# Contexts, Wk, Wv and turned rows read from DRAM by transfers over all 128 partitions

## The chip, the cores and the metric

The kernel runs on one core of a Trainium2 chip. The metric is device time in microseconds: the median of three executions, 770.59 us for the kernel before (770.08 to 770.86). A profile is of one execution more.

Names used below: TensorE (PE; its weight loads are PEld), VectorE (DVE), ScalarE (ACT), GpSimd (POOL), and SyncE (SP), which computes nothing and issues most of the DMA transfers. The transfers themselves are carried by the core's 16 DMA engines. SBUF is the on-chip memory of 128 partitions; PSUM takes TensorE's results.

## The reference

A layer of cross attention and then a feed-forward product, for 16 batches of 128 tokens with 1024 features, in float32:

```python
x = x + xattn(layernorm(x), ctx, ctx, Wq, bq, Wk, bk, Wv, bv, Wo, bo)   # 32 query heads, 8 key/value heads of 32
x = x + scale * (ei(layernorm(x)) @ kernel)    # kernel is 0/1; ei scales the last 20% of the features by -4
```

`xattn` is `Q = q Wq + bq`, `K = c Wk + bk`, `V = c Wv + bv`, per head `softmax(Q K^T / sqrt(32)) V`, and the result times `Wo` plus `bo`. Wq and Wo are 1024 x 1024, Wk and Wv 1024 x 256.

## The kernel before

**Work in groups of two batches.** There are eight groups. For each: K and V of the two contexts, Q of the two normalized x, attention in four parts (two batches, two halves of the heads), the output product with Wo and the residual, a second normalization, and the feed-forward product. From the second or third group on, the products Q, K with V, output and feed-forward are each made from seven products of half-size blocks (`seven`, L569) instead of eight, with sums and differences of the weights' blocks prepared once and kept in DRAM.

**Operands stand transposed.** The products need contexts and x with features on the partitions. VectorE's transpose instruction turns blocks of 32 x 32 (L445, L471, L983). So that a tile of tokens x features becomes features x tokens, the blocks must be placed beforehand: block (token block t, feature block k) has to lie in partitions 32k to 32k+31, at place t. A transfer from DRAM does that placing:

- `load_ctx` (L161) brings a context, 128 tokens x 1024 features, into a tile `[128 partitions, 4 token blocks, 8 chunks, 32]`.
- `through_dram` (L394) does the same for rows that the kernel has computed itself: it stores the normalized rows to DRAM (L409) and reads them back placed (L406). `rows_x` uses it for the queries of groups 2 to 7 (tiles `turn_x`), the output product's normalization for the feed-forward input of groups 0 to 6 (tiles `turn_f`). SyncE waits at L406 until the store has landed.
- `load_by_quadrants` (L169) loads Wv and Wk, whose rows are permuted in the same way.

Each of the three works by quadrant: one transfer per feature block k writes partitions 32k to 32k+31, over all four token blocks or several feature chunks at once. In all there are 16 contexts, 12 turned x and 14 turned f tiles of 512 KB in four transfers of 128 KB each, and Wv and Wk of 1 MB each. Every piece that is contiguous on both sides is 1 KB.

**The head.** Before anything can be computed, contexts 0 and 1, Wv and Wk are loaded by three queues in turn, SyncE, ScalarE and GpSimd (L201 to L205). Then SyncE loads x of batches 0 and 1 (L183), the bias bo, six pieces of Wq, contexts 2 and 3, and more. GpSimd makes the identity for TensorE's transposes and loads the small biases. TensorE's order is V of batch 0, V of batch 1, K of both, transposes of x, Q (L418, L434).

**The order of the rest** is written out by a small planner, class `Stream` (L24): generators yield pieces of TensorE's work with an estimated time, and other steps are filed for a later point of that clock (`later`). The resulting order on each engine is fixed at build time. SyncE's queue is served in order: a transfer that has to wait for a buffer or for a landing holds up all behind it. Weights of Wq, Wo and their sums come as pieces of 512 KB through a ring of 8 buffers (`fetch`, L238, issue at L243), each fetched when TensorE has used up an older one. The rows turned through DRAM share two buffers named `turn` with incoming x.

Of the kernel before, what the change touches and what calls it, by code (L numbers as in the profile page):

```python
# [95 lines left out]
def kernel(  # L96
# [16 lines left out]
    nc = tc.nc  # L113
# [7 lines left out]
    NC = D // P  # L121
# [21 lines left out]
    wk_sb = const.tile([P, NC, KV], FP, name="wk_sb")  # L143
    wv_sb = const.tile([P, NC, KV], FP, name="wv_sb")
# [13 lines left out]

    NB = P // 32

    def load_ctx(b, queues=(nc.sync,)):  # L161
        c_t = work.tile([P, NB, NC, 32], FP, tag="ctx", name=f"ctx{b}", bufs=2)
        src = key_value[b].rearrange("(t r) (k c f) -> k r t (c f)", r=32, k=NB, c=NC)
        for k in range(NB):
            dst = c_t[k * 32 : (k + 1) * 32].rearrange("r t c f -> r t (c f)")
            queues[k % len(queues)].dma_start(out=dst, in_=src[k])
        cs[b] = c_t

    def load_by_quadrants(dst, w, queues, *cuts):  # L169

        src = w.rearrange("(k c f) n -> k f c n", k=NB, f=32)
        n = 0
        for lo, hi in zip((0,) + cuts, cuts + (NC,)):
            for k in range(NB):
                queues[n % len(queues)].dma_start(
                    out=dst[k * 32 : (k + 1) * 32, lo:hi], in_=src[k][:, lo:hi]
                )
                n += 1

    def load_x(b, tag="row"):  # L180

        x_t = work.tile([P, D], FP, tag=tag, name=f"xn{b}", bufs=2)
        nc.sync.dma_start(out=x_t, in_=x[b])  # L183
        xns[b] = x_t
        if tag == "turn":
            turning.add(f"xn{b}")
# [11 lines left out]

    three = (nc.sync, nc.scalar, nc.gpsimd)  # L201
    load_ctx(0, three)
    load_by_quadrants(wv_sb, Wv, (nc.scalar, nc.gpsimd, nc.sync), 2, 4)
    load_ctx(1, three)
    load_by_quadrants(wk_sb, Wk, (nc.scalar, nc.gpsimd, nc.sync), 4)  # L205
    load_x(0)
    load_x(1)
    ident = const.tile([P, P], FP, name="ident")
# [185 lines left out]
    def through_dram(row, name, store, back, turn, then, tag="turn"):  # L394

        there = dram.tile([P, D], FP, name=f"dram_{name}")

        def load():
            bufs = 2 if tag == "turn" else TB
            c_t = work.tile([P, NB, NC, 32], FP, tag=tag, name=f"turn_{name}", bufs=bufs)  # L400
            if tag == "turn":
                turning.add(name)
            src = there.rearrange("(t r) (k n) -> k r t n", r=32, k=NB)
            for k in range(NB):
                dst = c_t[k * 32 : (k + 1) * 32].rearrange("r t c f -> r t (c f)")
                nc.sync.dma_start(out=dst, in_=src[k])  # L406
            stream.later(turn - back, lambda: then(c_t))

        stream.later(store, lambda: nc.sync.dma_start(out=there, in_=row) and None)  # L409
        stream.later(back, lambda: stream.when(lambda: tag != "turn" or len(turning) < 2, load))  # L410
# [718 lines left out]
    with tc.manual_schedule():  # L1129
# [17 lines left out]
        for j in range(GB):  # L1147
            load_ctx(GB + j)
# [83 lines left out]
        for grp in range(NGRP):  # L1232
# [39 lines left out]
            if not more:  # L1272
                for q in range(2 * NA):
                    b, a = grp * GB + q % GB, q // GB
# [6 lines left out]
            for q in range(2 * NA):  # L1281
                b, a = grp * GB + q % GB, q // GB
# [65 lines left out]
```

## Time and profile before

| | |
|---|---|
| Median of 3 executions | 770.59 us |
| Profiled execution | 765.46 us, of it 763.7 us from the first to the last instruction (the span) |
| TensorE busy | 746.6 us, 98% of the span |
| VectorE, ScalarE, GpSimd busy | 541.5, 380.2, 303.2 us |
| Moved by DMA | 203.36 MB, mean 266 GB/s over the span |
| SyncE's queue (q1) | 102480 packets, 200.31 MB, their time 81.8% of that of 16 engines |
| Granted TensorE clock | 1.00 throughout |

How to read the profile's views: a line of groups gives source line, engine, operation, tiles as out<-in, count, and busy time. A line of waits reads "who waited <- for what: us in total, times, longest us". The chain of waits is followed back from the last instruction, each line being start, duration and what it was. A row of DMA by stretch of time gives the packets in it, the bytes, and the mean rate. The DMA share is the time that packets took divided by that of 16 engines; it can exceed 1, because packets overlap on an engine.

### The profile page before, as it was taken

What the parts mean: (1) busy time and instruction counts of PE and PEld (TensorE: products, weight loads), DVE (VectorE), ACT (ScalarE), POOL (GpSimd) and SP (SyncE); (2) the same over time, 40 slices, a digit from 0 to 9 for tenths busy, and PEclk for the clock granted to TensorE, in tenths of its full rate; (3) what the DMA queues carried; (4) which work ended last, traced back from release to release, by engine and by line L of the source; (5) the groups of instructions that cost most, each with busy time, mean ns of one, the idle gap of its engine ahead of it and who ended that gap; (6) DMA issues with size and microseconds to landing.
All of it is one profiled execution on the core that took longest, in us unless ns stands there. A gap on an engine that the chain in (4) does not pass through costs nothing.

```text
span 763.7 us, 14898 instructions
## 1 busy us (share of the span) xinstructions
PE 746.6 (98%) x5232; PEld 563.4 (74%) x5232; DVE 541.5 (71%) x961; ACT 380.2 (50%) x1397; POOL 303.2 (40%) x356
## 2 busy tenths in 40 slices
PE   4999999999999999999999999999999999999997
PEld 3888884699747996489855998469984699546466
DVE  1456888977787667677676687865778766769586
ACT  0245764444735455344643447434464455568363
POOL 4069830342740146401652226322274113108582
PEclk9999999999999999999999999999999999999999
DMA  9989999989499895999779995899948988752912
GB/s 229 311 319 295 372 372 412 324 272 347 158 326 267 283 319 173 316 261 294 253 244 294 297 292 201 282 314 272 316 165 297 274 274 266 240 194 83 286 45 110
DMA packets 104314, 203.36 MB, mean 266 GB/s; under 512 B 8960, under 2 KB 58432, under 8 KB 104240
## 3 DMA queue, kind: packets, MB, share of 16 engines
q1 hardware_dynamic: 102480, 200.31, 81.8%
q10 hardware_dynamic: 1248, 1.11, 0.7%
q0 software_dynamic: 512, 0.99, 0.6%
q8 instruction: 41, 0.67, 0.4%
q14 instruction: 33, 0.27, 0.1%
HBM read 170.40 MB, written 31.98 MB: 265 GB/s over the span
## 4 chain that ended last, share of the span: by engine, by line
PE 90%; DVE 7%; DMA 2%; issue 1%; ACT 0%; SPq 0%; DVEq 0%
PE q_u L558 13%; PE o_u L862 12%; PE f_u L1017 7%; PE tpp L802 7%; PE q_v L558 7%; PE o_v L862 7%; PE k_u L558 5%; PE sc L769 4%; PE av L811 4%; PE q L418 4%; PE f_v L1017 3%; PE q_c L558 3%; PE k_v L558 3%; PE o_c L862 3%; PE f_c L1017 2%; PE k L418 2%
## 5 line engine op out<-in xcount | busy, mean ns | idle before, releaser
L785 ACT ACTIVATE p<-sc,negm 128x128 f32<-128x128 f32 x512 | 181.2, 370 | 147.3 <-DVE negm L781 73.1
L781 DVE TENSOR_REDUCE negm<-sc 128x4 f32<-128x512 f32 x128 | 86.9, 682 | 72.5 <-PE sc L769 72.5
L356 POOL CAST wide<-wf_sb 128x512 fp32r<-128x512 int8 x154 | 109.2, 749 | 64.0 <-PE f_u L1017 62.7
L804 ACT COPY pt<-tpp 128x512 f32<-128x512 f32 x128 | 75.1, 595 | 96.9 <-PE tpp L802 96.3
L797 DVE TENSOR_TENSOR p<-p,inv 128x512 f32<-128x512 f32 x128 | 103.4, 808 | 4.4
L785 ACT ACTIVATION_READ_ACCUMULATOR p<-sc,negm 128x1 f32 x512 | 106.3, 208 | 0.0
L196 POOL TENSOR_TENSOR x<-x,bo_b 128x256 f32<-128x256 f32 x64 | 50.3, 806 | 87.6 <-DMA x<-in_x_dram 74.9
L558 PE MATMUL q_u<-t,piece 128*128 128x128 f32 x672 | 81.3, 275 | 0.0
L558 PEld LDWEIGHTS q_u<-t,piece 128*128 128x128 f32 x672 | 78.1, 192 | 0.2 <-issue 0.2
L802 PE MATMUL tpp<-ident,p 128*128 128x128 f32 x512 | 75.9, 273 | 1.6 <-DVE p L797 1.6
L802 PEld LDWEIGHTS tpp<-ident,p 128*128 128x128 f32 x512 | 61.3, 141 | 20.1 <-issue 13.6
L862 PE MATMUL o_v<-piece,s 128*128 128x512 f32 x128 | 60.6, 601 | 0.2 <-DVE x L876 0.2
L862 PE MATMUL o_u<-piece,s 128*128 128x512 f32 x128 | 59.7, 597 | 0.5 <-DVE x L876 0.5
L862 PE MATMUL o_u<-piece,yT 128*128 128x512 f32 x128 | 58.6, 599 | 0.0
L819 ACT ACTIVATE yT<-av,bvT 128x512 f32<-128x512 f32 x32 | 22.0, 688 | 60.3 <-PE av L811 60.3
L769 PEld LDWEIGHTS sc<-kv,qT 32*128 32x128 f32 x1024 | 31.5, 186 | 25.7 <-issue 25.7
L374 POOL TENSOR_TENSOR rs_f<-ve_f,minus_half 128x1 f32<-128x1 f32 x16 | 9.5, 595 | 96.1 <-DVE ve_f L372 83.0
L961 POOL TENSOR_TENSOR s<-turn_f,turn_f 128x512 f32<-128x512 f32 x7 | 8.9, 1277 | 97.3 <-DVE turn_f L983 71.0
L354 ACT CAST wide<-wf_sb 128x512 fp32r<-128x512 int8 x70 | 43.2, 633 | 3.3 <-PE f_u L1017 3.0
L862 PEld LDWEIGHTS o_u<-piece,yT 128*128 128x128 f32 x128 | 23.5, 190 | 28.4 <-issue 26.7
L862 PEld LDWEIGHTS o_u<-piece,s 128*128 128x128 f32 x128 | 23.0, 190 | 27.6 <-issue 22.7
L862 PEld LDWEIGHTS o_v<-piece,s 128*128 128x128 f32 x128 | 22.4, 190 | 23.3 <-issue 18.9
(155 smaller groups left out, 1493.0 us busy)
## 6 DMA issues: line engine op xcount, KB each, us to landing
piece<-o SPq DMA_DIRECT2D x64, 512.0 KB, 4.8
piece<-q SPq DMA_DIRECT2D x56, 512.0 KB, 7.1
piece<-in_L_xattn_Wq_dram SPq DMA_DIRECT2D x50, 512.0 KB, 8.0
piece<-in_L_xattn_Wo_dram SPq DMA_DIRECT2D x48, 512.0 KB, 7.1
piece<-kv SPq DMA_DIRECT2D x18, 512.0 KB, 6.9
xn<-in_x_dram SPq DMA_DIRECT2D x16, 512.0 KB, 4.6
x<-in_x_dram SPq DMA_DIRECT2D x16, 512.0 KB, 5.1
ctx<-in_ctx_dram SPq DMA_DIRECT2D x60, 128.0 KB, 7.2
```

Of the source, the lines that this page charges most:

```text
L196: lambda cut=cut: nc.gpsimd.tensor_add(x_t[:, cut], x_t[:, cut], bo_b[:, cut]) and None,
L356: nc.gpsimd.tensor_copy(t, wf_sb[:, FFN[name], c])
L418: nc.tensor.matmul(mm, lhsT=lhsT, rhs=rhs, start=k == 0, stop=k == n - 1)
L558: nc.tensor.matmul(mm if part is None else mm[:, part], lhsT=lhsT, rhs=rhs, start=start and n == k == 0, stop=k == len(some) - 1, skip_gro ...
L769: nc.tensor.matmul(tiles[i][:, g], lhsT=qT[rows, g], rhs=kT[rows], start=True, stop=True,)
L781: nc.vector.tensor_reduce(negm, tile_, AX.X, ALU.max, negate=True)
L785: nc.scalar.activation(p[:, g], tile_[:, g], AF.Exp, bias=negm[:, g : g + 1], accum_out=total[:, g : g + 1],)
L797: nc.vector.tensor_mul(p, p, inv.unsqueeze(2).to_broadcast([P, NG, S]))
L802: nc.tensor.transpose(tp[:, g], p[:, g], ident)
L804: nc.scalar.copy(pt, tp)
L862: nc.tensor.matmul(mm, lhsT=lhsT[:, 2 * k + c], rhs=w[:, c], start=start and k == c == 0, stop=k == c == 1, skip_group_check=True,)
L1017: nc.tensor.matmul(mm, lhsT=part[:, c], rhs=w, start=start and c == n == 0, stop=c == HC - 1 and n == 1, skip_group_check=True,)
```

## The change

Contexts, turned rows, Wv and Wk are now read by transfers whose SBUF side is all 128 partitions. A context or a turned row has one transfer per token block t (four of 128 KB, as many as before), Wv and Wk one per feature chunk c (eight of 128 KB each; Wv had twelve, eight of 64 KB and four of 128 KB). The DRAM side of such a transfer is four blocks k of 32 rows of 1 KB. Which data ends up where in SBUF is the same, and the order of instructions on the compute engines is the same. The first loads are issued by SyncE and ScalarE in turn, GpSimd issues none of them any more.

```diff
+    def blocks_in(dst, src, queues=(nc.sync,)):
+        src = src.rearrange("(t r) (k n) -> t k r n", r=32, k=NB)
+        for t in range(NB):
+            queues[t % len(queues)].dma_start(
+                out=dst[:, t].rearrange("p c f -> p (c f)"), in_=src[t]
+            )
+
     def load_ctx(b, queues=(nc.sync,)):
         c_t = work.tile([P, NB, NC, 32], FP, tag="ctx", name=f"ctx{b}", bufs=2)
-        src = key_value[b].rearrange("(t r) (k c f) -> k r t (c f)", r=32, k=NB, c=NC)
-        for k in range(NB):
-            dst = c_t[k * 32 : (k + 1) * 32].rearrange("r t c f -> r t (c f)")
-            queues[k % len(queues)].dma_start(out=dst, in_=src[k])
+        blocks_in(c_t, key_value[b], queues)
         cs[b] = c_t
 
-    def load_by_quadrants(dst, w, queues, *cuts):
-
-        src = w.rearrange("(k c f) n -> k f c n", k=NB, f=32)
-        n = 0
-        for lo, hi in zip((0,) + cuts, cuts + (NC,)):
-            for k in range(NB):
-                queues[n % len(queues)].dma_start(
-                    out=dst[k * 32 : (k + 1) * 32, lo:hi], in_=src[k][:, lo:hi]
-                )
-                n += 1
+    def load_rows(dst, w, queues):
+
+        src = w.rearrange("(k c f) n -> c k f n", k=NB, f=32)
+        for c in range(NC):
+            queues[c % len(queues)].dma_start(
+                out=dst[:, c], in_=src[c]
+            )
...
-    three = (nc.sync, nc.scalar, nc.gpsimd)
-    load_ctx(0, three)
-    load_by_quadrants(wv_sb, Wv, (nc.scalar, nc.gpsimd, nc.sync), 2, 4)
-    load_ctx(1, three)
-    load_by_quadrants(wk_sb, Wk, (nc.scalar, nc.gpsimd, nc.sync), 4)
+    two = (nc.sync, nc.scalar)
+    load_ctx(0, two)
+    load_rows(wv_sb, Wv, two)
+    load_ctx(1, two)
+    load_rows(wk_sb, Wk, two)
...
-            src = there.rearrange("(t r) (k n) -> k r t n", r=32, k=NB)
-            for k in range(NB):
-                dst = c_t[k * 32 : (k + 1) * 32].rearrange("r t c f -> r t (c f)")
-                nc.sync.dma_start(out=dst, in_=src[k])
+            blocks_in(c_t, there)
             stream.later(turn - back, lambda: then(c_t))
```

## The prediction

> **What bounds the kernel now.** I read the page's busy times first, then the chain of waits, then the DMA rows by stretch of time.
>
> ```profile
> PE 746.6 (98%) x5232; PEld 563.4 (74%) x5232; DVE 541.5 (71%) x961; ACT 380.2 (50%) x1397; POOL 303.2 (40%) x356
> DMA  9989999989499895999779995899948988752912
> q1 hardware_dynamic: 102480, 200.31, 81.8%
> PE 90%; DVE 7%; DMA 2%; issue 1%; ACT 0%; SPq 0%; DVEq 0%
> ```
>
> TensorE is busy 746.6 of 763.7 us; only 17 us are left. But the DMA engines are nearly as full (the second line, tenths in 40 slices). So a faster transfer can gain little, while a slower one soon has TensorE waiting. The chain of waits says where those few DMA microseconds are:
>
> ```profile
> 2.12 5.02 DMA wv_sb<-in_L_xattn_Wv_dram
> 7.16 7.83 DMA ctx<-in_ctx_dram
> 15.88 3.72 PE v L418 x16
> 19.60 6.92 PE k L418 x32
> ```
>
> All in the head: the first product waits for Wv until 7.13, the second batch for its context until 15.06, then V, K, and Q from 28.6 us.
>
> Next the DMA rows: 20 to 29 us (Wq pieces: 1 KB runs into 128 partitions), 30 to 34 us (contexts: 1 KB runs into 32 partitions), 113 to 119 us (4 KB runs), and one round of the main loop, 300 to 387 us.
>
> ```profile
> DMA packets 3152, 3.15 MB, mean 350 GB/s; under 512 B 96, under 2 KB 3146, under 8 KB 3152
> ...
> DMA packets 932, 0.86 MB, mean 216 GB/s; under 512 B 105, under 2 KB 931, under 8 KB 931
> ...
> DMA packets 1109, 2.42 MB, mean 404 GB/s; under 512 B 105, under 2 KB 105, under 8 KB 1108
> ...
> DMA packets 12203, 23.92 MB, mean 275 GB/s; under 512 B 1008, under 2 KB 7152, under 8 KB 12194
> ```
>
> The size of a run is the same in the first two rows; the shape of the transfer alone makes 350 or 216 GB/s. At 350 GB/s each of 16 engines carries 21.9 GB/s.
>
> **The change, part by part.** It touches 46 tiles of 512 KB (524,288 bytes): 16 contexts, 12 x rows and 14 f rows back from DRAM, and Wv and Wk, two each. A context or turned row still takes four transfers of 128 KB, Wv now 8 instead of 12, Wk 8 as before. What changes is each transfer's shape. Before, both sides begin with 32 rows. After, the SBUF side begins with 128 partitions and the DRAM side with the 4 column blocks (`t k r n`, `c k f n`).
>
> *Price of one transfer.* No transfer of before begins with fewer than 32, so I bound it. Low end: 16 engines share it as they share a Wq piece, 131,072 / 350 GB/s = 0.37 us, a tile in 1.50 us; today it is 524,288 / 216 = 2.43 us, so a tile gains 0.93 us of DMA time. High end: four engines share it, a block each: 131,072 / (4 x 21.9) = 1.50 us, a tile in 6.0 us on engines that every other transfer also needs, 3.6 us more than now. I take the high end. A share that an engine can copy alone must be cut out of the outermost dimension of both sides. The two rows above show that this dimension decides the rate. 4 is all that the DRAM side offers, and the Wq pieces that give the low end begin with 128 on both.
>
> The Trainium skill, page "DMA: Bandwidth & Descriptors", section "Why a DMA increments its semaphore by 16 and not by 1", speaks against this change: the number of engines is the largest up to 16 that divides the slowest non-unit dimension of both patterns, which for 4 and 128 is 4. By that rule the sum is the 845 us below, by the Wq row it would be 765. No run here shows it yet.
>
> *Head.* 24 transfers (contexts 0 and 1, Wv, Wk) x 1.50 = 36 us from the first packets at 2.1 us: all of Wk at 38. x0 and x1 stand behind them on SyncE: at 404 GB/s 1.3 us each, so x0 lands at about 39.5. The two normalizations took from 20.05 to 26.43 on VectorE (6.4), transposes and copy to Q at 28.60 another 2.2: Q starts at 48.1, **+19.5 us**. K is no later: its last chunk lands at about 38 and the second half of K is 3.5 us. TensorE has nothing else to do, so all of it counts. GpSimd loses its nine transfers (about 5.1 us of issue) and builds the identity earlier; nothing waits for it before 26.13 us: 0. ScalarE issues 12 instead of 9 and SyncE 12 instead of 10 (the page of before has 0.3 to 0.45 us each, and they wait for earlier landings, as L175 and L166 do now). Behind ScalarE's stand its table load and the first K output, needed at 41 us in the new time: 0. Behind SyncE's stand x, bo and the Wq pieces, priced above.
>
> *28.6 to 150 us.* The table of stretches has a DMA share of 0.94, 1.00, 1.03 and 1.01 here: no idle engine time to spare. Four context tiles and the first turned rows, about 5.5 tiles x 3.6 = 20 us more on the four engines. Against it stand SyncE's waits for TensorE to free a piece buffer (6.6 us at 60 to 90, about 8 at 120 to 150) and the ring of 8 pieces. Ends 0 and 20; I take **+8**, nearer the row of waits.
>
> *Rounds of 87 us, five of them from 150 to 590 us.*
>
> ```profile
> 150.00:237.00 87.00, 86.52 (x631) 64.97 (x630) 65.27 (x118) 43.13 (x161) 38.13 (x46) 1.00 0.88 275
> 237.00:325.00 88.00, 88.00 (x664) 68.25 (x664) 63.09 (x115) 43.03 (x162) 33.52 (x41) 1.00 0.85 273
> 500.00:590.00 90.00, 89.54 (x670) 69.31 (x669) 64.67 (x119) 44.54 (x170) 33.46 (x41) 1.00 0.86 266
> 680.00:764.00 84.00, 78.22 (x341) 49.74 (x339) 62.67 (x100) 46.88 (x127) 46.31 (x59) 1.00 0.38 132
> ```
>
> (Columns: stretch, us, PE, PEld, DVE, ACT, POOL busy, clock, DMA share, GB/s.) A round moves 23.9 MB. Six tiles are 3.15; six Wq pieces, another 3.15, go at 350 GB/s, 9.0 us; 17.6 MB go at 404, 43.6 us. Those 52.6 us use all engines alike; on the four, six tiles add 36: **88.6 us in a round of 87**. TensorE can no longer hide them. And the four cannot be busy all the time: SyncE waits for each turned row's store before it loads it back and issues nothing meanwhile,
>
> ```profile
> SPq L406 <- DMA dram_f<-x2n: 9.3, 2, 7.1
> SPq L183 <- DVE x2l_s L933: 8.8, 1, 8.8
> SPq L406 <- DMA dram_x<-xq: 2.6, 1, 2.6
> ```
>
> (SyncE's waits, 300 to 387 us). Behind those L406 waits stand the next pieces of Wq, Wq's sums and Wo. I let a round have 7 us of such idle time: 95.6, about **+9 a round, +45 in all**. Ends: 0 (packets overlap as the 109.8% share at 20 to 29 us shows) and 6 x 3.6 = 21.
>
> *590 us to the end.* Four tiles in the first stretch: 21.5 MB / 404 = 53 us and 24 us, 77 of 90: +2. In the last, with a share of 0.38, two tiles: 0.
>
> Sum: 19.5 + 8 + 45 + 2 = 74.5. The profiled execution took 765.46 us, so 840; the median shown, 770.59, lies 5.1 us above it: **845 us**.
>
> **Rivals.**
> - *Faster: 16 engines share it after all.* For it: the Wq row. Against: the DRAM side's 4. The head's 24 transfers take 9 us: x1 by 14.7, norms 6.4, Q at about 23.5 instead of 28.6. Elsewhere TensorE is at 99 to 100% and 0.93 us a tile changes nothing: 770.6 - 5 = 765 (762 to 769). It decides if the first context's transfers land within 4 us and Wk by 14.
> - *Only the head is slower.* Four engines, but ring and slack cover the rounds: 770.6 + 19.5 = 790, with a few more 790 to 800. For it: SyncE's 8.8 us wait for a turning buffer, when queues run empty. Against: 88.6 us of transfers in 87.
> - *Nothing is hidden.* Head 19.5, the 40 tiles behind it 3.6 each: 770.6 + 19.5 + 144 = 934. Against: the ring's 8 pieces and the last 84 us.
> - *No change*: the transfers stay at 216 GB/s in another shape: 771.
>
> **How the numbers follow.** Four engines with rounds partly hidden (800 to 905): 0.74; head alone: 0.06; little or nothing hidden (905 to 934): 0.06; faster: 0.11; no change: 0.03. What a measurement of this kernel can tell from no change is about 0.2%, 1.5 us. The range 795 to 915 leaves out the faster and unchanged cases and both outer edges, 0.19. Faster 0.11, same 0.03, slower 0.86.
>
> **What would show it.** Right: in the head 1 KB packets at near 88 GB/s for some 35 us with a mean DMA share near 0.3, Q from about 48 us; TensorE waiting for pieces in each round, the DMA share falling while SyncE's waits for landings grow. Wrong: if the head's transfers run at 300 GB/s or more, the price of a transfer fails and everything with it; if rounds stay at 87 us after a late head, the cover of the ring was underrated; if rounds exceed 100 us, the idle time of the four engines was.

## The result, and the profile after

The kernel after takes 906.66 us (median of six executions, 903.68 to 909.57) against 769.76 us (768.19 to 770.86) before: a ratio of 1.1777, 95% interval 1.1746 to 1.1807. The forecast was 845 us with a range of 795 to 915. So the sign and the range held, and the size was 62 us short.

Medians and ratios leave out executions more than 1.5% above the fastest of their kernel, which was one, of the f rows (819.17 us, below). From here on all numbers are of profiled executions unless a median is named. The profile of the kernel after has a span of 906.1 us in a run of 907.91; before it was 763.7 in 765.46. First the page's busy times, granted clock in 40 slices (tenths of full speed), SyncE's queue and shares of the chain:

```profile
PE 784.1 (87%) x5232; PEld 588.8 (65%) x5232; DVE 545.9 (60%) x961; ACT 381.8 (42%) x1397; POOL 297.0 (33%) x347
...
PEclk9899989998899989999899997999989999999989
...
q1 hardware_dynamic: 100832, 200.70, 66.9%
...
PE 50%; DMA 32%; DVE 9%; SPq 5%; issue 2%; POOL 1%; DVEq 0%; POOLq 0%
```

The 142.4 us that the span grew by are of two kinds. TensorE stands idle for 122 us instead of 17 (+105). And the same 5232 records of matrix products take 784.1 us instead of 746.6 (+37.5): the granted clock is no longer 1.00 everywhere, its mean is 0.957, and 4.3% of 906 us is 39 us. SyncE's queue moves the same bytes (200.70 MB against 200.31) in a smaller share of the engines' time (66.9% against 81.8%), and yet the chain now runs through DMA for 32% of the span instead of 2%.

Next the table of stretches (stretch, us, PE, PEld, DVE, ACT, POOL busy, clock, DMA share, GB/s), for the head and for one round of the kernel after, then a round of the kernel before, and the DMA row of the kernel after for 2 to 34 us:

```profile
0.00:30.00 30.00, 9.66 (x18) 5.11 (x19) 2.92 (x5) 1.28 (x1) 3.26 (x11) 1.00 0.25 82
...
370.00:479.50 109.50, 94.40 (x671) 72.96 (x667) 65.43 (x118) 44.72 (x170) 33.25 (x41) 0.95 0.69 224
```

```profile
298.00:389.00 91.00, 91.00 (x676) 69.80 (x672) 65.60 (x119) 44.54 (x170) 33.49 (x41) 1.00 0.85 271
```

```profile
DMA packets 3079, 3.32 MB, mean 104 GB/s; under 512 B 222, under 2 KB 2952, under 8 KB 3079
```

A share of 0.25 while little but these loads is under way fits four engines of sixteen; in slices of 0.8 us, from 10 to 31 us, the rate stands at 95 to 97 GB/s. In the round, PE is busy 94.4 of 109.5 us at a clock of 0.95, where before it was busy 91.00 of 91.00 us at 1.00.

Where the span grew, by the first scores of each of the eight groups (before, at 42.5, 114.9, 206.6, 298.0, 389.2, 480.4, 571.6 and 651.3 us; after, at 65.8, 148.2, 260.5, 370.0, 480.5, 589.6, 698.9 and 783.5):

| Stretch | before, us | after, us | difference |
|---|---|---|---|
| head | 42.5 | 65.8 | +23.3 |
| group 0 | 72.4 | 82.5 | +10.1 |
| groups 1 to 5, each | 91.1 to 91.7 | 109.1 to 112.3 | +17.9 to +20.6, together +94 |
| group 6 | 79.7 | 84.6 | +4.9 |
| group 7 to the end | 112.4 | 122.6 | +10.2 |

The head, by the chain of waits (start, duration, what):

```profile
0.74 4.18 DMA ctx<-in_ctx_dram
4.94 14.82 DMA wv_sb<-in_L_xattn_Wv_dram
19.78 10.97 DMA wk_sb<-in_L_xattn_Wk_dram
30.78 9.96 DMA xn<-in_x_dram
```

At 30.78 us the chain reaches the issue of x, which lands at 40.74; Q starts at 51.85 instead of 28.60.

A round, again by the chain of waits:

```profile
421.14 10.79 DMA dram_f<-x2n
...
434.31 7.86 DMA dram_f<-x2n
...
444.49 9.15 DMA piece<-q
...
453.78 4.37 PE q_v L556 x24
```

This is the order of SyncE's queue. It stores a normalized row, has to wait until the landing, 10.8 us after the issue (eight transfers of contexts were issued just ahead of it, from 406.43 to 418.69), and issues the four loads of that row, the store of the next row and, at 434.90, two pieces of Wq's sums. Then it waits for the second landing, 7.9 us after that store's issue, issues four more loads, and only then, at 444.49, the next two pieces, of which the first takes 9.15 us. TensorE's timeline shows what that costs (start, duration, what; in brackets the idle time ahead of it and what ended it), and behind it the same twelve records of before:

```profile
443.52 2.90 PE L556 MATMUL q_u<-t,piece 128*128 128x128 f32 x12 [7.83 <-DMA piece<-q]
...
453.78 4.37 PE L556 MATMUL q_v<-xT,piece 128*128 128x128 f32 x24 [4.10 <-DMA piece<-q]
```

```profile
359.58 1.50 PE L558 MATMUL q_u<-t,piece 128*128 128x128 f32 x12
```

There are two waits, the first for the pieces issued at 434.90, the second for those issued at 444.49. Behind the first one twelve records take 2.90 us where they took 1.50 before: half pace. The round that precedes this one has the same pair of waits, 7.75 and 2.92 us. The waits of the whole run (who waited for what: us in total, times, longest us), and behind them the one of SyncE for the same stores in the kernel before:

```profile
SPq L164 <- DMA dram_f<-x2n: 89.5, 13, 9.9
...
DVE turn_f L981 <- DMA turn_f<-dram_f: 111.8, 14, 13.9
...
PE q_u L556 <- DMA piece<-q: 51.1, 10, 8.0
...
PE q_v L556 <- DMA piece<-q: 18.6, 9, 4.1
```

```profile
SPq L406 <- DMA dram_f<-x2n: 45.5, 12, 7.1
```

Before, TensorE waited for no piece. The pieces themselves were not changed; they are late.

### The profile page after: what moved, and what is told of

The parts are those of the page before. It is cut to its first block, busy times and chain, and to the rows that moved or that the text cites. A ratio compares the mean times of both kernels' runs of the same rounds, so it can differ in the third digit from the quotient of the medians.

```text
span 906.1 us, 14881 instructions
## 1 busy us (share of the span) xinstructions
PE 784.1 (87%) x5232; PEld 588.8 (65%) x5232; DVE 545.9 (60%) x961; ACT 381.8 (42%) x1397; POOL 297.0 (33%) x347
## 3 DMA queue, kind: packets, MB, share of 16 engines
q1 hardware_dynamic: 100832, 200.70, 66.9%
## 4 chain that ended last, share of the span: by engine, by line
PE 50%; DMA 32%; DVE 9%; SPq 5%; issue 2%; POOL 1%; DVEq 0%; POOLq 0%
DMA dram_f<-x2n 13%; PE o_u L860 6%; PE q_u L556 6%; DMA piece<-q 5%; PE f_u L1015 5%; PE o_v L860 5%; SPq L164 5%; PE tpp L800 4%; PE q_v L556 4%; PE k_u L556 4%; PE f_v L1015 3%; PE av L809 3%; PE sc L767 3%; DMA turn_f<-dram_f 2%; PE k_v L556 2%
## 5 line engine op out<-in xcount | busy, mean ns | idle before, releaser
L556 PE MATMUL q_u<-t,piece 128*128 128x128 f32 x672 | 95.6, 303 | 51.1 <-DMA piece<-q 51.1
L556 PEld LDWEIGHTS q_u<-t,piece 128*128 128x128 f32 x672 | 91.1, 217 | 52.9 <-DVE inv L794 43.2
L802 ACT COPY pt<-tpp 128x512 f32<-128x512 f32 x128 | 75.0, 594 | 112.3 <-PE tpp L800 111.3
L981 DVE STREAM_TRANSPOSE turn_f<-turn_f 128x512 f32<-128x512 f32 x28 | 19.1, 697 | 111.8 <-DMA turn_f<-dram_f 111.8
L800 PE MATMUL tpp<-ident,p 128*128 128x128 f32 x512 | 79.3, 282 | 4.4 <-DVE inv L794 2.5
L800 PEld LDWEIGHTS tpp<-ident,p 128*128 128x128 f32 x512 | 64.1, 146 | 23.7 <-issue 16.5
L860 PE MATMUL o_v<-piece,s 128*128 128x512 f32 x128 | 62.9, 620 | 9.0 <-DVE x L874 9.0
L443 DVE STREAM_TRANSPOSE cT<-ctx 128x512 f32<-128x512 f32 x32 | 21.9, 694 | 44.7 <-DMA ctx<-in_ctx_dram 44.7
L556 PE MATMUL q_v<-xT,piece 128*128 128x128 f32 x224 | 32.6, 305 | 17.8 <-DMA piece<-q 15.2
L375 POOL TENSOR_TENSOR rs_f<-ve_f,minus_half 128x1 f32<-128x1 f32 x16 | 9.6, 597 | 111.1 <-DVE ve_f L373 95.2
```

What stands on the lines that cost most here:

```text
L556: nc.tensor.matmul(mm if part is None else mm[:, part], lhsT=lhsT, rhs=rhs, start=start and n == k == 0, stop=k == len(some) - 1, skip_gro ...
L800: nc.tensor.transpose(tp[:, g], p[:, g], ident)
L802: nc.scalar.copy(pt, tp)
L860: nc.tensor.matmul(mm, lhsT=lhsT[:, 2 * k + c], rhs=w[:, c], start=start and k == c == 0, stop=k == c == 1, skip_group_check=True,)
```

## The experiments

### The price of one transfer, by itself

A kernel without the computation (only loads of 8 x 128 KB in runs of 1 KB, and a copy by VectorE when all eight have landed). The DRAM side begins with n blocks; n is varied:

```python
        part = rows[256 * i : 256 * (i + 1)]
        if n == 128:
            return part[:128]
        return part.rearrange("(a q r) n -> q a r n", a=n, q=2)[0]
...
            queues[i % len(queues)].dma_start(out=t[:, i], in_=rows_of(n, i))
```

> Only loads of 128 KB in runs of 1 KB from x, eight to a stretch, each stretch ended by a copy on VectorE, twice over; the layer is not computed. The DRAM side of a stretch is 128 equal rows, then quadrants (32 partitions, 4 token blocks, the shape of before), then 16 blocks of 8 rows, 8 of 16, 4 of 32 (the shape of after), 4 of 32 issued by SyncE and ScalarE in turn, 2 of 64; the SBUF side is 128 partitions in all but the quadrants. Theory, the number of engines is what divides both sides' outermost counts: near 350 GB/s for 128 rows and for 16 blocks, 216 for quadrants, 175 for 8 blocks, 96 for 4, the same 96 for 4 by two queues, 48 for 2. Rival, blocks of DRAM rows are slow in themselves or a queue is the limit: 16 and 8 blocks already near 100, or two queues nearer 190.

VectorE's timeline of this run, first for 16, 8, 4, 4 by two queues, and 2 blocks, then 128 rows and quadrants (the bracket holds the wait for the eight loads):

```profile
23.63 1.23 DVE L114 COPY u<-t 128x2048 f32<-128x2048 f32 x1 [7.25 <-DMA t<-in_x_dram]
33.87 1.23 DVE L114 COPY u<-t 128x2048 f32<-128x2048 f32 x1 [9.01 <-DMA t<-in_x_dram]
48.90 1.23 DVE L114 COPY u<-t 128x2048 f32<-128x2048 f32 x1 [13.80 <-DMA t<-in_x_dram]
63.99 1.23 DVE L114 COPY u<-t 128x2048 f32<-128x2048 f32 x1 [13.87 <-DMA t<-in_x_dram]
89.77 1.23 DVE L114 COPY u<-t 128x2048 f32<-128x2048 f32 x1 [24.55 <-DMA t<-in_x_dram]
97.46 1.23 DVE L114 COPY u<-t 128x2048 f32<-128x2048 f32 x1 [6.47 <-DMA t<-in_x_dram]
105.40 1.23 DVE L121 COPY u<-t 128x2048 f32<-128x2048 f32 x1 [6.71 <-DMA t<-in_x_dram]
```

Moved in those stretches: 16 blocks 195 to 196 GB/s, 8 blocks 144 to 148, 4 blocks 87 to 89, 2 blocks 46; 128 rows 210 to 217, quadrants 209 to 217. The median packet of 1 KB took 46 ns in each stretch but one (quadrants the second time, 64 ns). From 8 blocks to 4 and from 4 to 2 the rate falls to 0.6 and 0.52; a second issuing queue changes nothing (13.87 against 13.80). For 128 rows and 16 blocks the expectation had 350, and it was missed: SyncE needs 3.7 us for its eight issues, and the loads moved in 4.8 to 5.4 us, so the issuing is probably a limit there. Quadrants were as fast as 128 rows here, but since these too stay far below 350 GB/s, this run does not tell what quadrants can do at most. One thing the trace adds, from the records of the semaphores: a landing wrote its semaphore 16 times for 128 rows, quadrants and 16 blocks alike, and 9, 5 and 3 times for 8, 4 and 2 blocks. That fits one update by each engine and one more where there are fewer than 16. The prediction's high end, 88 GB/s, is confirmed, and the rival of 16 engines falls.

The Trainium skill, page "DMA: Bandwidth & Descriptors", section "Why a DMA increments its semaphore by 16 and not by 1", has the number of engines as the largest up to 16 that divides the slowest non-unit dimension on both sides; 8, 4 and 2 blocks at 146, 88 and 46 GB/s agree with it.

### Head alone and loop alone

Before, with the change for contexts 0 and 1, Wv, Wk and the two queues only (head), or for everything else only (loop):

```diff
# head
+        if b < GB:
+            blocks_in(c_t, key_value[b], queues)
+            cs[b] = c_t
+            return
...
+    load_rows(wv_sb, Wv, two)
...
+    load_rows(wk_sb, Wk, two)
# loop
+        if b >= GB:
+            blocks_in(c_t, key_value[b], queues)
+            cs[b] = c_t
+            return
...
+            blocks_in(c_t, there)
```

> The kernel before, with the first loads alone (contexts 0 and 1, Wv, Wk) as in the change. Theory, the head's loss only shifts what follows: 769.8 plus the 23.3 us by which the first scores are later in the profile after (42.5 to 65.8), 793 us (789 to 798), rounds of 91.2 us as before. Rival, a late head puts SyncE's queue out of step and part of the longer rounds comes from it: above 805.

> The kernel before, with contexts 2 to 15 and the turned rows as in the change and the head as before. Theory: rounds of 109 to 111 us as after, 906.7 - 23.3 = 883 us (876 to 891). Rival, the head makes the rounds late: under 860.

Head alone: 791.90 against 768.85, 1.0300 [1.0274, 1.0327], +23.1 us; its rounds stay at 91.1 to 92.6 us. A late head only shifts what follows. Loop alone: 882.27, 1.1458 [1.1413, 1.1503], +113.4 us. Together 136.5, and the whole change 136.9: within these intervals the two do not touch each other.

### Contexts, turned rows, turned f rows

The loop divided further, each from before: only the 14 contexts behind the head, only the 26 turned rows, only the 14 f rows.

```diff
# contexts
+        if b >= GB:
+            blocks_in(c_t, key_value[b], queues)
...
# turned rows
+            blocks_in(c_t, there)
# f rows
+            if name[0] == "f":
+                blocks_in(c_t, there)
...
```

> The kernel before, with contexts 2 to 15 alone as in the change (14 tiles). Theory A, the four engines' time is what runs out: two such tiles leave 52.6 + 2 x 5.5 + 4 x 2.4 = 73 us of transfers in a round of 91, so nearly all is hidden: 770 to 785. Theory B, it is the place in SyncE's queue (the store of the rows for the feed-forward stands behind eight slow context transfers, the load waits for the store, pieces of Wq's sums stand behind the load): 6 to 10 us a round, 800 to 830.

> The kernel before, with the turned rows alone as in the change (26 tiles). Theory A: 52.6 + 4 x 5.5 + 2 x 2.4 = 79 us of transfers in a round of 91, nearly all hidden: 770 to 795, and with the contexts alone far less than the two together. Theory B, the contexts cause the waits: little here, 770 to 790. Rival, each slow transfer costs its 3 us wherever it stands: 26 x 3 = 78, 848.

> The kernel before, with the rows for the feed-forward product alone (turn_f, 14 of the 26 turned tiles) read back as in the change. Theory: VectorE takes these rows in order among its other work and stands waiting for them (111.8 us in the profile after), so they carry most of the 76 us of all turned rows: 825 to 840. Rival, each slow tile costs the same: 769.8 + 14 x 2.9 = 811.

| Changed | tiles | median, us | ratio | us more | per tile |
|---|---|---|---|---|---|
| contexts | 14 | 799.96 | 1.0400 [1.0359, 1.0441] | 30.1 | 2.2 |
| f rows | 14 | 815.10 | 1.0555 [1.0492, 1.0619] | 42.7 | 3.1 |
| turned rows, x and f | 26 | 846.15 | 1.0997 [1.0948, 1.1047] | 76.3 | 2.9 |
| all three | 40 | 882.27 | 1.1458 [1.1413, 1.1503] | 113.4 | 2.8 |

For the f rows the three times behind the ratio lie far apart (804.86, 815.10 and 816.16), so the difference is taken from the ratio, 5.55% of 770.14; its interval is 37.9 to 47.7.

The theory that I had held, time on the four engines that runs out at the end of a round, needs losses that are small for a part and large for the whole: contexts alone leave the four engines far from full. It fails: contexts cost 30 us by themselves, and contexts and turned rows together, 30.1 + 76.3 = 106.4, come to nearly the 113.4 of both. The second theory for the contexts, the place in SyncE's queue, had 800 to 830 and is just met, but for the turned rows it had 770 to 790. The loss goes by tiles, at nearly the whole price of one, as the rival for the turned rows (848) and that for the f rows (811) had it; the theory for the f rows (825 to 840) failed. As an estimate, at 96 GB/s a tile takes 524,288 bytes / 96 GB/s = 5.46 us against 2.43 before, 3.03 more; 2.2 to 3.1 of it arrives at the end. By difference the 12 x rows cost 33.6, 2.8 each, which the intervals do not tell from the f rows' 3.1.

The waits of the run with only turned rows changed, of SyncE and of TensorE, and behind it those with only contexts changed:

```profile
SPq L164 <- DMA dram_f<-x2n: 76.6, 13, 7.2
...
PE q_u L562 <- DMA piece<-q: 26.1, 5, 6.8
PE q_v L562 <- DMA piece<-q: 14.7, 5, 3.5
```

```profile
SPq L417 <- DMA dram_f<-x2n: 60.7, 11, 10.0
...
PE q_u L569 <- DMA piece<-q: 15.7, 6, 3.9
```

With contexts alone, the loads behind the store have their old shape, and yet SyncE waits 15 us longer for the same store than before: it is the store that is late, when slow loads have been issued ahead of it.

### 128 partitions without the four blocks

Turned rows only. The store now does the placing, in four transfers of 32 partitions, so that a load over 128 partitions reads 128 equal rows of DRAM:

```diff
+                nc.sync.dma_start(
+                    out=c_t[:, t].rearrange("p c f -> p (c f)"),
+                    in_=there[:, t * (D // NB) : (t + 1) * (D // NB)],
+                )
...
+            dst = there.rearrange("(k r) (t n) -> t r k n", k=NB, t=NB)
+            for t in range(NB):
+                nc.sync.dma_start(
+                    out=dst[t], in_=row[t * 32 : (t + 1) * 32].rearrange("r (k n) -> r k n", k=NB)
+                )
```

> The kernel before, with turned rows read back by four transfers over 128 partitions as in the change, but from a scratch laid out so that the DRAM side is 128 equal rows of 1 KB; the placing is done by the store, in four transfers of 32 partitions. Theory: all engines share such a load, so nothing is lost, 765 to 775. Rival, loads over 128 partitions in that place are slow in themselves: as slow as the turned rows of the change.

768.35 us, 0.9976 [0.9956, 0.9996]. All 128 partitions on the SBUF side cost nothing, with the stores in four transfers too; the four blocks on the DRAM side were the whole of the 76 us. SyncE's wait for the f stores fell too:

```profile
SPq L404 <- DMA dram_f<-x2n: 19.9, 12, 3.8
```

19.9 us instead of 45.5, and the time moved by less than 2: with pieces in time, that wait had cost little.

### Weights alone over 128 partitions, and the whole change with 16 engines

First Wv and Wk alone, from an order in DRAM in which 128 rows follow each other (laid out in that order before the launch, as Wq and Wo already are), by the three old queues. Then the whole change in this way: contexts and weights laid out before the launch, turned rows as in the last experiment, first loads by SyncE and ScalarE.

```diff
+        src = w.rearrange("(c p) n -> c p n", p=P)
...
             queues[t % len(queues)].dma_start(
...
+                out=c_t[:, t].rearrange("p c f -> p (c f)"),
+                in_=key_value[b][:, t * (D // NB) : (t + 1) * (D // NB)],
             )
```

> The kernel before, with Wv and Wk handed over in an order of rows in which each feature chunk is 128 equal rows in DRAM, loaded by eight transfers each over 128 partitions, by the same three queues; the rest as before. Theory: 2 MB of the head at 350 instead of about 235 GB/s, 3 us less until K, 765 to 768. Rival, the head waits for the second context whatever the weights do: 769 to 771.

> The change with a DRAM side that all 16 engines can share: contexts, Wk and Wv handed over in an order of rows in which each of the change's transfers (four a context, eight a weight, SyncE and ScalarE in turn for the first) reads 128 equal rows of 1 KB; turned rows placed by the store as in e_relaid. Theory, the loss is the number of engines alone and TensorE is the bound beyond the head: 24 first transfers in about 9 us instead of 13, Q some 4 to 5 us sooner, 764 to 767. Rival, loads over 128 partitions gain nothing in the head (as with Wv and Wk alone): 768 to 771.

Weights alone: 770.03 us, 1.0004 [0.9984, 1.0024], as the rival had it; the head now waits for the contexts, 10.1 us in two waits, where before it waited 7.6 us for Wv and 2.1 for the second context. All of it: 764.66 against 770.14, 0.9928 [0.9908, 0.9948], 5.5 us faster than the kernel before and 142 us faster than the kernel after. TensorE is busy 747.6 us of its profile, and its wait in the head is this:

```profile
PE v L432 <- DMA wv_sb<-in_L_xattn_Wv_dram: 6.7, 1, 6.7
```

TensorE's long waits in the head are now one of 6.7 us (before 7.1 for Wv and 2.1 for the second context), Q starts at 25.86 instead of 28.60, and the rounds stay at 91.3 to 91.7. The prediction's rival of 16 engines had 765 (762 to 769). Its head gains 2.7 us in the profile, though, not the 5 that the rival counts on; where the rest of the 5.5 us comes from was not settled.

### What makes the pieces late: VectorE or SyncE's queue

VectorE stood 111.8 us at the transposes of f rows, and could have held up TensorE in that way. In the kernel after, these transposes are filed 8 us later in the plan:

```diff
-    FBACK = ((7.0, 18.0), (8.0, 19.0))
+    FBACK = ((7.0, 26.0), (8.0, 27.0))
```

> The kernel after, with VectorE's transposes of the rows for the feed-forward filed 8 us later on the planner's clock (18 and 19 become 26 and 27 us behind the start of the rows' way through DRAM); the transfers are the same, one store and one load of x rows move by one place in SyncE's queue. Theory, the loss in a round is that VectorE, ScalarE and then TensorE stand behind rows that are not there yet: most of the 7.8 us wait of the fifth product of Q goes, and the half clock behind it; SyncE's waits for the stores, 4 to 6 us a round, stay: 907 - 5 x 8 to 11, 850 to 880. Rival, the four engines' time is what runs out: 895 or more.

935.35 us, 1.2149 [1.2095, 1.2203], 28.7 more than the kernel after. The theory fails. The time lies in the rival's range (895 or more), but the four engines' load was not changed, so the 28.7 us do not speak for it. The waits tell more:

```profile
DVE turn_f L981 <- DMA turn_f<-dram_f: 27.4, 6, 4.9
...
SPq L164 <- DMA dram_f<-x2n: 84.8, 13, 10.0
SPq L184 <- DVE x2l_s L931: 70.8, 5, 15.4
...
PE q_u L556 <- DMA piece<-q: 46.3, 9, 7.9
```

VectorE's standing is three quarters gone, and TensorE's wait for the pieces is still 46.3 us. So VectorE was not the cause of that wait; SyncE's wait for the store stayed with it. What is lost is new: the turned buffers come free later, and SyncE waits 70.8 us (42.8 before this edit) to load the next x. The rounds grow to 113.2 to 115.7 us and the last part from 122.6 to 132.5; that SyncE's wait for the buffers is the cause of all of this is not shown.

Put side by side, the three quantities go together in most kernels:

| Kernel | SyncE's wait for f stores, us | TensorE's wait for `piece<-q` in q_u and q_v, us | rounds, us |
|---|---|---|---|
| 128 equal rows, turned | 19.9 | 0 | 91.1 to 95.2 |
| before | 45.5 | 0 | 91.1 to 91.7 |
| head alone | 49.3 | 0 | 91.1 to 92.6 |
| contexts | 60.7 | 19.1 | 94.4 to 98.1 |
| turned rows | 76.6 | 40.8 | 102.5 to 109.8 |
| after, transposes later | 84.8 | 60.0 | 113.2 to 115.7 |
| loop alone | 87.8 | 65.7 | 106.5 to 113.3 |
| after | 89.5 | 69.7 | 109.1 to 112.3 |

Up to 49 us of it in the run TensorE waits for no piece (2.0 us with the weights alone, where SyncE's wait is 45.5). Each microsecond beyond the 45.5 of before goes with 1.3 to 1.6 us of waiting by TensorE (19.1 for 15.2, 40.8 for 31.1, 69.7 for 44.0). The f rows have less, 22.4 us for 26.1, in the profile of their longest execution. In the kernel with the filler, below, SyncE waits 90.6 us and TensorE for pieces only 10.5, because the filler takes up that time.

How much of the lateness is SyncE's order (issue behind a wait) and how much is the longer way of the pieces themselves can be read for one round, in SyncE's timeline of before and of after:

```profile
328.41 9.69 SPq L166 DMA_DIRECT2D ctx<-in_ctx_dram  x8
...
339.62 0.38 SPq L409 DMA_DIRECT2D dram_f<-x2n  x1
...
347.69 1.74 SPq L406 DMA_DIRECT2D turn_f<-dram_f  x4
...
350.01 1.23 SPq L243 DMA_DIRECT2D piece<-q  x2
```

```profile
406.43 12.26 SPq L164 DMA_DIRECT2D ctx<-in_ctx_dram  x8
...
421.14 0.38 SPq L407 DMA_DIRECT2D dram_f<-x2n  x1
...
431.99 2.22 SPq L164 DMA_DIRECT2D turn_f<-dram_f  x4
...
434.90 1.20 SPq L244 DMA_DIRECT2D piece<-q  x2
```

Counted from the issue of the first context, the two pieces go out after 28.5 us instead of 21.6. Of these 6.9 us, 3.5 lie ahead of the store, 2.8 in the wait for its landing and 0.6 in the issues behind it. From issue to landing the first of them then takes 8.5 us instead of 5.9. So in this round nearly three quarters of the lateness is late issue. What I did not try is to issue the pieces from another engine's queue, so what that order alone costs the whole run stays open.

### The half clock

Two attempts. First the kernel after with 16 products more in each of five rounds, issued where TensorE waits, to keep its clock up:

```diff
+                if prod == "s3 t3" and 2 <= grp < NGRP - 1:
+                    fill = ps_tp.tile([P, HALF], FP, tag="tp", name=f"fill{grp}")
+                    for _ in range(16):
+                        nc.tensor.matmul(fill, lhsT=ident, rhs=bo_b[:, :HALF], start=True, stop=True)
```

> The kernel after, with 16 matmuls of the identity and bo (128x512, their result is never read) put ahead of the fifth product of Q in groups 2 to 6, where TensorE stands idle 7.5 to 8.0 us in each round after: about 7.2 us of added work a round. Theory, the idle time also costs a stretch at half the TensorE clock (6.8 to 10.2 us recorded at 0.5 right behind it, worth half of that): the added work fits in the wait and keeps the clock up, 3 us gained in each of five rounds, 892 us (886 to 900). Rival, the clock is no part of the loss: 907 if all of the added work fits in the wait, up to 940 if none does.

949.76 us, 1.2358 [1.2315, 1.2401], 43 more than the kernel after, outside both expectations:

```profile
PE fill L635 <- ACT pt L806: 37.0, 5, 7.6
...
458.86 16.96 PE L635 MATMUL fill<-bo_b,ident 128*128 128x512 f32 x32 [7.46 <-ACT pt L806]
```

The filler's own result buffer was not free, so TensorE waited up to 7.6 us ahead of the filler instead of behind it, and the half clock fell on the filler. It was also twice as long as priced: 15.7 to 17.0 us a round, not 7.2. By the next run, where 48 such products take 41.47 us, 16 take 13.8 at full clock. The mean clock stayed at 0.959. So this run does not tell what a clock that is kept up would gain.

Then the effect by itself: streams of 48 matrix products (two records each in the trace) and no transfer near them, with a chain of VectorE operations of growing length between one stream and the next (no part of the computation).

> Only TensorE and VectorE: ten streams of 48 float32 products of 128x512 on the same operands, between them 1, 2, 3, 4, 5, 7, 9, 12 and 15 VectorE operations on 128x512 (about 0.7 us each) that the next stream waits for; the layer is not computed. Theory, taken from the profile after (waits of 2.9 to 8 us are each followed by 3.4 to 10.2 us at a granted clock of 0.5, waits of 1 to 2 us by none): streams behind waits over some 3 us run their first 3 to 10 us at half pace, those behind shorter ones do not. Rival, the half clock comes with the load on DMA and memory: clock 1.0 throughout.

TensorE's timeline (in brackets the idle time ahead):

```profile
221.16 41.47 PE L110 MATMUL mm<-g 128*128 128x512 f32 x96 [2.96 <-DVE g L112]
266.32 43.16 PE L110 MATMUL mm<-g 128*128 128x512 f32 x96 [3.69 <-DVE g L112]
314.62 43.47 PE L110 MATMUL mm<-g 128*128 128x512 f32 x96 [5.14 <-DVE g L112]
```

Idle times up to 2.96 us cost nothing beyond themselves (41.47 us also behind 0.78, 1.51 and 2.23 us); from 3.69 us on each costs the next stream 1.7 to 2.6 us more. Idleness alone does it, without DMA load.

Yet in the kernel after a wait of 2.92 us (ahead of 343.17) was followed by half clock, so the length of a wait does not decide it. The records of the clock in the traces do: they change only at steps of 3.41 us, and what counts is TensorE's idle time within one such step. Over all thirteen kernels in which the clock was recorded, 75 steps that began at full clock held 2.0 us or more of idle time, and half clock followed each of the 75; of 2745 steps with less, it followed four (1.6 to 1.9 us of idle time). The wait of 2.92 us had 2.4 us in one step, and that of 2.96 us was cut into 1.5 and 1.5. The Trainium skill, page "TensorE: Matmul & The Clock Gate", part 1, puts the drop to half speed after an idle window of about 3.4 us that runs freely; the free-running window agrees, but here 2.0 us of idle time within one were enough.

## Why the prediction was right and wrong

**Price of a transfer (6.0 us a tile): right, one of its reasons not.** 95 to 97 GB/s in the head, 88 in the measurement by itself; a DMA share of 0.25. Both of the prediction's tests for it held. But it took from the rows of 350 and 216 GB/s that the outermost dimension decides the rate. Both shapes land with 16 updates of the semaphore, so these two rows do not differ by a number of engines, and what makes 216 of 350 in the kernel before stays open. The conclusion, four engines for four blocks, was right all the same.

TensorE's 5232 records have the same order in both kernels, so the delay can be read at each of them. At the prediction's borders it is 23.3 us (28.6 us of before), 33.3 (150 us), 127.9 (590 us) and 142.4 at the end.

**Head (+19.5): right, 4 us small.** Measured +23.3 in the profile and +23.1 by the run with the head alone; Q at 51.85, not 48.1. x landed at 40.74 (39.5 was said). That alone, with the 8.6 us of normalization and transposes, would have put Q at 49.3. What failed is "K is no later": the last of Wk landed at 44.0, not 38. TensorE waits for it, and the two queues' traffic shows why (q10 is ScalarE's; 22 to 30 us, then 34 to 42 us):

```profile
44.04 5.72 PE L416 MATMUL k<-cT,wk_sb 128*128 128x256 f32 x18 [4.19 <-DMA wk_sb<-in_L_xattn_Wk_dram]
...
q10 hardware_dynamic: 388, 0.39, 13.7%
...
q1 hardware_dynamic: 1230, 1.92, 84.7%
q10 hardware_dynamic: 211, 0.21, 9.7%
```

The sum let x wait for all of Wk. But x stands only behind SyncE's half of it; from 30.78 us on SyncE's x, bo and Wq pieces went beside ScalarE's last Wk transfers, whose traffic fell to about half. K ends at 49.8, the transposes of x stand behind it on TensorE, and Q starts another 2.1 us later.

**28.6 to 150 us (+8): right.** Measured +10.0.

**Rounds (+9 each, +45): the step that failed.** They grew by 17.9 to 20.6; from 150 to 590 us it is +94.6, 50 more than said, which is most of the 62 us that the forecast was short. Its working set 88.6 us of transfers against a round of 87 and let the four engines be idle for 7 us. Two errors stand in it. A round of before is 91.3 us long by the first scores and moves 24.8 MB; with the prediction's own rates that is 90.7 us of transfers, so by capacity alone six slow tiles would just have fitted. And, by the same estimate, the four engines are idle not for 7 but for about 109.5 - 90.7 = 19 us of a round, as the prediction's last sentence on wrongness had it. The cause is in its own remark that the next pieces stand behind L406's waits. It priced those waits as they were. But a store that follows slow loads lands later, so the wait itself grows (10.8 and 7.9 us from issue to landing in one round, 8.1 and 3.9 before; 89.5 against 45.5 us of waiting over the run), the issues ahead of it take longer too, and the pieces come too late for TensorE. The rival "nothing is hidden" (3.6 us a tile) describes the loop better: 2.8 us a tile were measured.

**A term that was missing: the clock.** Of the 19 us that a round grew by on average, some 14 are idle time and 4.5 are busy time, at half clock behind it. Over the whole run the longer busy time is 37.5 of 142.4 us; no row of before showed it, with a granted clock of 1.00 throughout.

**590 us to the end (+2 and 0): wrong by 12.** Measured +14.5. Group 6 grew by 4.9, the last part by 10.2. In the last part the low DMA share was taken as cover, but two f rows lie on the path there: VectorE stands 14.6 us for them (5.2 before), the residual is late, and TensorE waits 7.5 us for it; 2.6 us are longer busy time.

**Range and chances.** 906.66 us lies inside 795 to 915, but 2 us beyond the case that the prediction favoured, rounds partly hidden, 800 to 905 (0.74). It lies in "little or nothing hidden", 905 to 934, which had 0.06. That the range held is in part luck: its upper end reached 10 us into that case.

**Rivals.** Sixteen engines: falls for this change, but gives the right time (765) for the kernel in which sixteen do share. Only the head: falls, the loop alone costs 113.4. Nothing hidden (934): falls in its full form, 2.8 of 3.6 us a tile came. No change: falls.

## What to carry to other kernels

Count what the outermost dimension of a transfer offers on both sides before its width on either: here 128 partitions were read by four engines, since the DRAM side began with four blocks. When transfers get slower, a sum of engine time per round is only a lower bound; follow the in-order queue that issues them, look for waits for a landing in it, and ask what stands behind these. And where TensorE will wait for 2 us or more at a time, count the slow products after the wait too.

## What was unexpected of the hardware

- Half clock follows 2.0 us of idle time of TensorE within one step of 3.41 us, whether the wait is longer than that or not (75 of 75 steps).
- SyncE's issues of the context transfers became slow too: at least 0.53 us each and 1.31 in the median, instead of 0.31 and 0.31, so eight of them hold its queue for 12.3 us (from 406.43 on) where eight held it for 9.7 before (from 328.41 on). The turned f loads of the same shape, issued right behind a wait, took 0.51 us.
- A wait of 3.7 us of TensorE costs 1.7 us more behind it, and one of 8.8 us hardly more, 1.8 us; 2.6 us was the most, behind 6.6.
